# Moving one load, one pair of weights and one convolution in a fused graph layer on one core

## Chip, core and metric

The kernel runs on one core of one Trainium2 chip. The metric is the device time of one execution in microseconds (us), the median of seven executions: 1859.76 us before the change, between 1858.95 and 1863.57. All arithmetic is in f32.

## What is computed

There are 32 graphs of 512 nodes with 256 features each, and a dense 0/1 adjacency for each graph. The reference, cut to what matters:

```python
h = relu(layernorm(x))                                   # [32, 512, 256]
# convolution branch, channels first
c = relu(bn1(conv1(h.T)))                                # 256 -> 256, one tap
c = bn2(conv2(c))                                        # 256 -> 256, 17 taps
x_conv = relu(c + h.T).T
# message branch
s   = h @ w_se.T + b_se                                  # 3 numbers per node
A   = exp(-dist2(s, s)) * adj                            # [512, 512] per graph
msg = relu(h @ w_msg.T + b_msg)
x_nmp = A @ msg
# GRU cell on [x_conv, x_nmp] with state h
r, z = sigmoid(gi_r + gh_r), sigmoid(gi_z + gh_z)
n = tanh(gi_n + r * gh_n)
out = x + (1 - z) * n + z * h
```

## The kernel before

The 32 graphs are worked in two **groups** of 16 (`GB = 16`, `NG = 2`). conv2 is done in the frequency domain: each graph is cut into 8 windows, a group gives 128 windows, and each of 40 **units** (two of the 80 rows of a spectrum) is a product of the windows' spectrum with conv2's transformed weights. Each group goes through two stages, and a late stage over pairs of graphs (inverse transform, GRU gates, output) follows both:

1. `first_part(g, ...)`, lines 799 to 868. For each graph b: load x (`load_x`, line 116); `statistics` (line 280: four bn_stats, four aggregates and one addition on DVE, a power of -0.5 on POOL for the reciprocal deviation); `normalise` (four tensor_scalar on DVE, line 296); `transpose_h` (line 302: eight PE transposes named phT, two DVE copies into hT at line 308, a store of hT to HBM, called hd, at line 309); `conv1` (line 312: 16 matmuls named pc, two DVE additions at line 323, two ACT relus at line 324); `windows_to_freq` (matmuls named px). In group one, conv2's weights are transformed between the graphs (`weights_to_freq`: matmuls named pw, copies named wst on DVE and ACT, stores to wd in HBM). The loop runs ahead of itself: in turn b it does the statistics of b + 2, the transposes of b + 1, the normalisation of b + 2, and then conv1 of b.
2. `nodes(g, ...)`, lines 905 to 940, the **node loop**. It goes over the group's graphs, the last one first. For each graph: reload hT (`load_h`), rearrange it on ACT (`by_chunks`, tile hq), `message` (matmuls named pm, DVE additions), `features` (small DVE operations into the tiles fl and fr), `factors` (PE transposes named psl and psr), `affinity` (matmuls named pd, exp on ACT, DVE transposes of adj at line 471 and products at line 472 into A), `aggregate` (16 matmuls named pn), and a store (`save_nmp`, named nd). Between them go the units: `prepare` (POOL: one sum of the weights, wsum, line 351, and two of the spectra, both, lines 364 and 365) and `product` (12 matmuls named py, copy and sums into y, store yd on ACT's queue). Of group one's 40 units the loop does 36; the last four, 36 to 39, are **left over** and are done at the head of `first_part(1, ...)`, in the list `left`, whose five entries are run by `fill()`.

What sets the order of the work around the change:

- `first_part` stands under `tc.manual_schedule()`: each engine issues its instructions in the order of the code. `nodes` does not: there the framework's planner orders each engine's instructions by program order and by its own estimate of when each is ready, and may pull an instruction forward over many others.
- Loads of x 16 (group two's first graph), adj, hT and the units' weights (wt) all go through SP's queue, as do the stores of hT; yd and nd go through ACT's queue. A queue is served in order. Each transfer of SP and ACT is given the next of eight semaphores in turn, and is not issued before the last transfer on that semaphore has landed, whichever engine issued it.
- Tiles have few buffers: three for wt, so unit 38's weights can be loaded once unit 35's product is done; two for adj; two for hT.
- x 16 has a buffer of its own (pool "ahead"). In the code its load stands in front of the node loop (line 943), and its statistics behind the loop (line 946).

Of the kernel before, what the change touches and what calls it, by code (L numbers as in the profile page):

```python
# [65 lines left out]
def gnn_layer(  # L66
# [24 lines left out]
    GB = P // W  # L91
    NG = B // GB
# [23 lines left out]
    def load_x(b, queue=nc.sync):  # L116
        X[b] = pools["ahead" if b == GB else "first"].tile([P, NC, D], FP, tag="x", name=f"x_{b}", bufs=1 if b == GB else 3)
        queue.dma_start(X[b], x[b].rearrange("(c p) d -> p c d", p=P))
# [47 lines left out]
    def batch_norm(k, scale, shift, engine):  # L166
        engine.tensor_scalar(scale, at[k + "_v"], BN_EPS, None, op0=ALU.add)
        nc.gpsimd.tensor_tensor(scale, scale, minus_half[:, :DC], op=ALU.pow)
        engine.tensor_mul(scale, scale, at[k + "_g"])
        engine.tensor_mul(shift, at[k + "_m"], scale)  # L170
        engine.tensor_sub(shift, at[k + "_b"], shift)
# [28 lines left out]
    def shift_w1():  # L200
        nc.scalar.copy(shift1_row.rearrange("p (i q) -> p i q", i=DC), by_parity(row1[1][:, :D]))
# [78 lines left out]
    def statistics(b):  # L280
        stats = work.tile([P, NC, 6], FP, tag="stats", name=f"stats_{b}")
        mv = work.tile([P, NC, 2], FP, tag="mv", name=f"mv_{b}")
        for c in range(NC):
            nc.vector.bn_stats(stats[:, c, :], X[b][:, c, :])  # L284
        for c in range(NC):
            nc.vector.bn_aggr(mv[:, c, :], stats[:, c, :])
        rstd = work.tile([P, NC], FP, tag="rstd", name=f"rstd_{b}")
        STATS[b] = mv, rstd
        nc.vector.tensor_scalar(rstd, mv[:, :, 1], LN_EPS, None, op0=ALU.add)
        nc.gpsimd.tensor_tensor(rstd, rstd, minus_half[:, :NC], op=ALU.pow)  # L290
# [508 lines left out]
    def first_part(g, freq, between, left=()):  # L799


        b0, b1 = g * GB, (g + 1) * GB
        for b in range(b0, b0 + 3):
            if b not in X and (g == 0 or b == b0):
                load_x(b)
        if g == 0:
            t = XN[b0] = pools["first"].tile([P, NC, D], FP, tag="xn", name="rows", bufs=2)
            ones, diags = t[:, 0, :P], t[:, 1:3, :].rearrange("p i (c m) -> p i c m", m=P)
            nc.vector.memset(ones, 1.0)
            batch_norm("bn1", scale1, shift1, nc.gpsimd)  # L810
            bn1_row(0, scale1, ones, diags)
            bn1_row(1, shift1, ones, diags)
        if b0 not in STATS:
            statistics(b0)
        normalise(b0)
        if g == 0:
            scale_w1()
            shift_w1()
        else:
            load_x(b0 + 1)  # L820
            load_x(b0 + 2)
        left = list(left)

        def fill():
            for step in left.pop(0) if left else ():
                step()

        fill()
        transpose_h(b0)
        fill()  # L830
        statistics(b0 + 1)
        normalise(b0 + 1)
        fill()
        for b in range(b0, b1):
            if b + 3 < b1:
                load_x(b + 3, nc.gpsimd)
            if b == b0:
                conv1(b)
                if g == 0:
                    for steps in between(0):  # L840
                        for step in steps:
                            step()
                fill()
            if b + 2 < b1:
                statistics(b + 2)
            if b + 1 < b1:
                transpose_h(b + 1)
            if b + 2 < b1:
                normalise(b + 2)
            if b == b0:  # L850
                fill()
                xf = freq(g)
            one, two = between(b - b0) if b > 0 else ([], [])
            if b > b0:
                conv1(b)
            if b == b1 - 1:
                load_h(b0)
            for step in one:
                step()
            if b > b0:  # L860
                windows_to_freq(b - 1, xf)
            for step in two:
                step()
        by_chunks(b1 - 1)
        load_h(b0 + 1)
        windows_to_freq(b1 - 1, xf)
        by_chunks(b0)
        return xf
# [8 lines left out]
    with tc.tile_pool(name="freq", bufs=1) as fpool:  # L877
        def freq_tile(g):
            return fpool.tile([P, DC, L, P], FP, tag="xf", name=f"xf_{g}")

        with phase("first", "gen"):
            gen = pools["gen"]
            per = N // D
            steps = [partial(weights_to_freq, gen, pc, i) for pc in range(QI // PI) for i in range(0, PI, per)]
            load_w1()
            load_x(0)
            load_x(1)
            load_taps(gen, 0, nc.sync)

            def between(b):  # L890
                if b % 2 == 0 and b // 2 + 1 < QI // PI:
                    load_taps(gen, b // 2 + 1)
                if 1 <= b <= len(load_weights):
                    load_weights[b - 1]()

                mine = spread(steps, b, GB - 1) if b < GB - 1 else [partial(load_unit, 0, u) for u in range(3)]
                return mine[:1], mine[1:]

            with tc.manual_schedule():
                xf = first_part(0, freq_tile, between)  # L900


        LEFT = 4

        def nodes(g, xf, units, last):


            b1 = (g + 1) * GB
            todo = [b1 - 1] + list(range(g * GB, b1 - 1))
            def begin(i):  # L910
                if i < GB:
                    if todo[i] not in HQ:
                        by_chunks(todo[i])
                    message(todo[i])
                    features(todo[i])

            load_adj(todo[0])
            begin(0)
            factors(todo[0])
            begin(1)  # L920
            affinity(todo[0])
            for i, b in enumerate(todo):
                mine = spread(units, i, last) if i < last else []
                more = i + 1 < GB
                if i + 2 < GB and todo[i + 2] not in HT:
                    load_h(todo[i + 2])
                if more:
                    load_adj(todo[i + 1])
                    factors(todo[i + 1])
                for u in mine[:1]:  # L930
                    product(pools["pw"], g, u, xf)
                begin(i + 2)
                if more:
                    affinity(todo[i + 1])
                for u in mine[1:2]:
                    product(pools["pw"], g, u, xf)
                aggregate(b)
                save_nmp(b)
                for u in mine[2:]:
                    product(pools["pw"], g, u, xf)  # L940

        with phase("pw", "ahead"):
            load_x(GB)
            with phase("nodes"):
                nodes(0, xf, range(UNITS - LEFT), GB)
                statistics(GB)
            with phase("first", "sums"):
                combine = combine_weights()

                def between(b):  # L950

                    if b == GB - 3:
                        for u in range(3):
                            load_unit(1, u)
                    two = [partial(sum_unit, pools["pw"], 1, b - GB + 3)] if b > GB - 3 else []
                    return combine[b - 2] if 1 < b < len(combine) + 2 else [], two


                pw, (u0, u1, u2, u3) = pools["pw"], range(UNITS - LEFT, UNITS)
                left = [[],  # L960
                        [partial(prepare, pw, 0, u1, xf), partial(product, pw, 0, u0, xf), partial(load_unit, 0, u2)],
                        [partial(product, pw, 0, u1, xf), partial(load_unit, 0, u3), partial(prepare, pw, 0, u2, xf)],
                        [partial(prepare, pw, 0, u3, xf), partial(product, pw, 0, u2, xf)],
                        [partial(product, pw, 0, u3, xf)]]
                prepare(pw, 0, u0, xf)
                load_unit(0, u1)
                with tc.manual_schedule():
                    xf = first_part(1, freq_tile, between, left)
            with phase("nodes"):
                nodes(1, xf, range(UNITS), GB - 3)  # L970
# [76 lines left out]
```

## Time and profile before

| | |
|---|---|
| median of seven executions | 1859.76 us |
| the profiled execution | 1860.62 us |
| its span, first to last instruction | 1858.8 us |
| mean granted clock of PE | 0.992 |
| group one, first part (0 to 172 us) | PE busy 159.01 us, DMA share 0.88 |
| group one, node loop (172 to 469) | PE busy 291.35 of 297, DMA share 0.78 |
| group two, first part (469 to 592) | PE busy 118.64 of 123, DMA share 0.61 |
| group two, node loop (592 to 892) | PE busy 297.17 of 300, DMA share 0.83 |
| late stage (892 to the end) | PE busy 957.00 of 966.8, DMA share 0.35 |

PE is the matmul engine, DVE the vector engine, ACT the scalar engine, POOL the engine that does the units' sums, SP the engine that only issues transfers. In a timeline each row has its start and duration in us, the engine, the line of the code, the operation, what is written from what is read, the number of instructions merged, and in brackets how long the engine had been idle and who released it. In a table of windows each row has the window, its length, the busy time of PE, weight loads, DVE, ACT and POOL, then PEclk (the mean clock granted to PE, 1.00 is full speed), the DMA engines' share and GB/s.

### The profile page before, as it was taken

The numbers are of one execution on the slowest core, as the hardware profiler recorded it, in microseconds if no ns is written. First come the engines' busy times: TensorE is split into PE (matmuls) and PEld (weight loads), VectorE is DVE, ScalarE is ACT, GpSimd is POOL, SyncE is SP. The second block draws the span as 40 slices with busy tenths as digits, with TensorE's granted clock in tenths as the row PEclk, the third lists the DMA queues.
The fourth block names the chain that finished last, engine by engine and source line by source line (L and its number), as shares of the span: only waits on it lengthen the run. The fifth ranks groups of instructions, "written<-read, shape, count | busy, mean of one in ns | idle before, by whom it ended". The sixth has DMA issues, their size and how long they took to land.

```text
span 1858.8 us, 20075 instructions
## 1 busy us (share of the span) xinstructions
PE 1823.2 (98%) x6598; PEld 1090.1 (59%) x6598; DVE 1111.7 (60%) x2234; ACT 577.7 (31%) x1075; POOL 586.4 (32%) x565
## 2 busy tenths in 40 slices
PE   7999999999999999999999999999999999999998
PEld 5776666666798666666555544555455544555443
DVE  6875565555696564555165566645665466645666
ACT  3455444332145433333222212222122212222121
POOL 3331243343442344444413322132213322132221
PEclk9999999999999999999999999999999999999999
DMA  8998888866567988768513442244422442244312
GB/s 222 297 261 243 208 241 238 221 178 187 191 232 215 223 263 238 222 198 248 165 55 65 119 119 85 39 114 119 111 65 62 119 119 85 40 113 119 111 24 52
DMA packets 307451, 289.25 MB, mean 156 GB/s; under 512 B 148028, under 2 KB 237148, under 8 KB 306964
## 3 DMA queue, kind: packets, MB, share of 16 engines
q1 hardware_dynamic: 281300, 224.22, 45.3%
q10 hardware_dynamic: 19024, 38.68, 5.8%
q0 software_dynamic: 7024, 25.07, 4.8%
q8 instruction: 53, 0.87, 0.2%
q14 instruction: 50, 0.41, 0.1%
HBM read 191.50 MB, written 96.40 MB: 155 GB/s over the span
## 4 chain that ended last, share of the span: by engine, by line
PE 93%; DVE 2%; issue 2%; DMA 1%; POOL 1%; ACT 0%; POOLq 0%; ACTq 0%; SPq 0%; DVEq 0%
PE pg L585 29%; PE pn L585 14%; PE pn L480 12%; PE py L385 11%; PE pc L320 6%; PE pm L431 6%; PE pc L573 5%; PE px L335 4%; PE pw L256 2%; PE pd L466 2%; PE phT L307 2%; PE psr L455 1%; DMA x<-in_x_dram 1%; DVE stats L284 0%; DMA hT<-hd 0%
## 5 line engine op out<-in xcount | busy, mean ns | idle before, releaser
L480 PE MATMUL pn<-A,msg 128*128 128x512 f32 x512 | 225.0, 592 | 0.0
L585 PE MATMUL pg<-hp,sw 128*128 128x512 f32 x434 | 221.8, 593 | 0.7 <-DVE rz L604 0.5
L585 PE MATMUL pg<-np,sw 128*128 128x512 f32 x434 | 221.6, 592 | 0.0
L585 PE MATMUL pg<-cp,sw 128*128 128x512 f32 x434 | 221.6, 592 | 0.0
L563 POOL TENSOR_TENSOR hp<-hp 128x512 f32<-128x512 f32 x64 | 80.9, 1275 | 412.9 <-DMA hp<-hd 321.8
L364 POOL TENSOR_TENSOR both<-xf 128x256 f32<-128x256 f32 x78 | 60.9, 781 | 330.1 <-PE py L385 296.1
L480 PEld LDWEIGHTS pn<-A,msg 128*128 128x128 f32 x512 | 97.1, 190 | 110.6 <-issue 107.7
L385 PE MATMUL py<-wt,both 128*128 128x256 f32 x624 | 152.3, 387 | 4.0 <-POOL both L365 3.3
L563 POOL TENSOR_TENSOR cp<-cp 128x512 f32<-128x512 f32 x64 | 80.4, 1268 | 233.8 <-ACT cp L579 232.5
L600 ACT ACTIVATE rz<-rz,brz 128x512 f32<-128x512 f32 x93 | 67.0, 721 | 260.2 <-DVE rz L604 260.2
L392 DVE TENSOR_TENSOR y<-y,py 128x256 f32<-128x256 f32 x78 | 31.8, 408 | 193.5 <-ACT y L391 193.5
L585 PEld LDWEIGHTS pg<-hp,sw 128*128 128x128 f32 x434 | 82.2, 190 | 104.8 <-issue 98.3
L585 PEld LDWEIGHTS pg<-cp,sw 128*128 128x128 f32 x434 | 82.5, 190 | 103.8 <-issue 103.8
L585 PEld LDWEIGHTS pg<-np,sw 128*128 128x128 f32 x434 | 82.5, 190 | 103.8 <-issue 103.8
L385 PEld LDWEIGHTS py<-wt,both 128*128 128x128 f32 x624 | 115.1, 192 | 46.9 <-issue 27.6
L472 DVE TENSOR_TENSOR A<-e,at 128x512 f32<-128x512 f32 x128 | 112.4, 917 | 39.3 <-ACT e L469 38.9
L351 POOL TENSOR_TENSOR wsum<-wt 128x512 f32<-128x512 f32 x78 | 108.2, 1388 | 52.3 <-DMA wt<-wd 43.6
L320 PE MATMUL pc<-w,hT 128*128 128x256 f32 x512 | 121.1, 391 | 0.7 <-DVE hT L308 0.7
L723 ACT ACTIVATE nt<-nt,vech 128x512 f32<-128x512 f32 x64 | 46.2, 722 | 235.8 <-DVE nt L722 235.8
L431 PE MATMUL pm<-wmsg,hq 128*128 128x259 f32 x512 | 117.6, 382 | 1.0 <-ACT hq L417 1.0
L585 PE MATMUL pn<-cp,sw 128*128 128x512 f32 x224 | 114.4, 592 | 0.0
L585 PE MATMUL pn<-hp,sw 128*128 128x512 f32 x224 | 114.4, 592 | 0.0
(141 smaller groups left out, 2956.1 us busy)
## 6 DMA issues: line engine op xcount, KB each, us to landing
wt<-wd SPq DMA_DIRECT2D x160, 256.0 KB, 4.1
adj<-in_adj_dram SPq DMA_DIRECT2D x128, 256.0 KB, 5.6
wd<-wst SPq DMA_DIRECT2D x64, 320.0 KB, 5.2
yd<-y ACTq DMA_DIRECT2D x80, 256.0 KB, 4.0
yt<-yd SPq DMA_DIRECT2D x30, 640.0 KB, 7.4
hd<-hT SPq DMA_DIRECT2D x32, 512.0 KB, 3.9
nd<-nmp ACTq DMA_DIRECT2D x32, 512.0 KB, 3.8
xb<-in_x_dram SPq DMA_DIRECT2D x128, 128.0 KB, 3.7
```

The lines of the kernel that those rows point to most:

```text
L320: nc.tensor.matmul(p[:, j, :], HT[b][:, ic, c * P : (c + 1) * P], w1[:, ic, :], start=(ic == 0), stop=(ic == DC - 1))
L335: nc.tensor.matmul(p[:, j * 2 * L : (j + 1) * 2 * L], H1[b][:, c0 + j, ic * P : (ic + 1) * P], fwd, start=True, stop=True)
L351: nc.gpsimd.tensor_tensor(t, WT[g, u][:, 0], WT[g, u][:, 1], op=ALU.add)
L364: nc.gpsimd.tensor_tensor(both[:, 0], re, im, op=ALU.add)
L385: nc.tensor.matmul(dst, v[:, ic, :], w[:, ic, :], start=(ic == 0), stop=(ic == DC - 1))
L431: nc.tensor.matmul(p[:, : D + NS], hq[:, ic, c * P : (c + 1) * P], wmsg[:, ic, :], start=(ic == 0), stop=(ic == DC - 1))
L472: nc.vector.tensor_mul(A[b][:, mc, :], e, at)
L480: nc.tensor.matmul(p, MSG[b][:, mc, dc * P : (dc + 1) * P], A[b][:, mc, :], start=(mc == 0), stop=(mc == NC - 1))
L563: nc.gpsimd.tensor_tensor(t[:, dst, :], t[:, a, :], t[:, b, :], op=sub)
L573: nc.tensor.matmul(bk[:, t0:t1], YT[p][j][:, c, oc * P : (oc + 1) * P], back[:, n : n + t1 - t0], start=(c == 0), stop=(c == len(spans) - ...
L585: nc.tensor.matmul(bk[:, t], sw[:, k, q, o, :], terms[k][q][:, t], start=(first and i == 0), stop=(i == len(ks) - 1), skip_group_check=True)
L600: nc.scalar.activation(rz[:, g, j, :], src, AF.Sigmoid, bias=brz[:, g : g + 1], scale=1.0)
```

## The change

Three things are moved; no instruction is added or removed.

1. The load of x 16 goes from in front of the node loop into it, at its ninth turn (`i == GB // 2`), and its statistics go from behind the loop to the thirteenth turn (`i == 3 * GB // 4`).
2. In the list of left-over work, the load of unit 38's weights (`u2`) goes from the second entry into the first, which runs before the first transposes of group two and so before the first store of hT.
3. In group one's first part, conv1 of the second graph (b = 1) goes from behind the transposes of graph 2 and the normalisation of graph 3 to the beginning of its turn.

```diff
@@ first_part
                 fill()
+            if g == 0 and b == b0 + 1:
+                conv1(b)
             if b + 2 < b1:
                 statistics(b + 2)
             if b + 1 < b1:
...
             one, two = between(b - b0) if b > 0 else ([], [])
-            if b > b0:
+            if b > b0 + (g == 0):
                 conv1(b)
@@ nodes
                 more = i + 1 < GB
+
+                if g + 1 < NG and i == GB // 2:
+                    load_x(b1)
+                if g + 1 < NG and i == 3 * GB // 4:
+                    statistics(b1)
@@ the stages
-            load_x(GB)
             with phase("nodes"):
                 nodes(0, xf, range(UNITS - LEFT), GB)
-                statistics(GB)
...
-                left = [[],
-                        [partial(prepare, pw, 0, u1, xf), partial(product, pw, 0, u0, xf), partial(load_unit, 0, u2)],
+                left = [[partial(load_unit, 0, u2)],
+                        [partial(prepare, pw, 0, u1, xf), partial(product, pw, 0, u0, xf)],
```

## The prediction

> **What bounds the kernel.** I began with the page's busy line, went on to the waits of PE, and then to the timeline of each wait the diff touches.
>
> ```profile
> PE 1823.2 (98%) x6598; PEld 1090.1 (59%) x6598; DVE 1111.7 (60%) x2234; ACT 577.7 (31%) x1075; POOL 586.4 (32%) x565
> ```
>
> PE is busy 1823.2 of 1858.8 us, so nothing is won but by closing its gaps, 35.6 us in all, and the half-speed matmuls that follow some of them. The waits of PE (us in total, times, longest) name the gaps:
>
> ```profile
> PE psl L450 <- DVE fr L445: 5.7, 3, 3.7
> PE phT L307 <- DVE xn L296: 4.6, 2, 3.5
> PE py L385 <- POOL both L365: 3.3, 1, 3.3
> ```
>
> The longest of each row stands where one edit of the diff lies. **Gap A** (timeline, start and duration in us): after graph 1's transposes PE sits 3.53 us until xn of graph 2 is there, although graph 1's hT is complete at 23.99 and its conv1 waits behind the transposes.
>
> ```profile
> 22.71 1.28 DVE L308 TENSOR_SCALAR hT<-phT 128x512 f32<-128x512 f32 x2
> 24.57 2.30 PE L307 MATMUL phT<-ident,xn 128*128 128x128 f32 x8 [3.53 <-DVE xn L296]
> 26.67 5.47 PE L320 MATMUL pc<-w,hT 128*128 128x256 f32 x16
> ```
>
> **Gap B**, at the head of the first node loop: the load of x 16 leaves at 176.08 and takes 7.8 us; the planner put its bn_stats into the middle of graph 0's message additions; DVE stands there 3.93 us, and the features that psl needs come behind it.
>
> ```profile
> 176.08 0.43 SPq L118 DMA_DIRECT2D x<-in_x_dram  x1
> 183.88 0.43 DVE L284 BATCH_NORM_STATS2 stats<-x 128x6 f32<-128x256 f32 x1 [3.93 <-DMA x<-in_x_dram]
> 185.91 0.44 PE L450 MATMUL psl<-ident,fl 128*128 128x128 f32 x1 [3.66 <-DVE fr L445]
> ```
>
> **Gap C**, at the head of group two: the weights of unit 38 leave SP only at 474.76, behind h's store at 474.32; POOL waits 2.41 us for them, PE 3.28 us for POOL.
>
> ```profile
> 474.32 0.34 SPq L309 DMA_DIRECT2D hd<-hT  x1
> 474.76 2.49 SPq L347 DMA_DIRECT2D wt<-wd  x4
> 479.19 1.27 POOL L351 TENSOR_TENSOR wsum<-wt 128x512 f32<-128x512 f32 x1 [2.41 <-DMA wt<-wd]
> 481.88 3.78 PE L385 MATMUL py<-wt,both 128*128 128x256 f32 x8 [3.28 <-POOL both L365]
> ```
>
> **What a gap costs beyond itself.** Windows of the gap and of the stretch behind it (us, then the engines' busy time, PEclk, DMA share, GB/s):
>
> ```profile
> 182.20:185.90 3.70, 0.04 (x4) 0.03 (x1) 2.02 (x12) 1.77 (x4) 0.00 (x0) 0.75 1.21 201
> 185.90:190.40 4.50, 4.50 (x13) 3.79 (x14) 1.05 (x7) 1.90 (x5) 1.02 (x1) 0.50 1.22 193
> 478.60:481.90 3.30, 0.02 (x2) 0.02 (x1) 1.58 (x3) 1.23 (x2) 2.71 (x4) 0.86 0.59 224
> 481.90:487.30 5.40, 5.40 (x13) 4.22 (x14) 0.00 (x0) 0.00 (x0) 3.31 (x4) 0.50 0.28 97
> ```
>
> The granted clock is 0.50 behind both. From the mean clock inside a gap I get when it fell: B 1.8 us after PE went idle (0.75 = 1 - 0.5 x 1.85/3.7), C 2.4 us, A 2.6 us. Behind the 0.98 us wait at 209.14 it stays 1.00. So a gap near 1 us is free of it, one over 3 us is not.
>
> **Gap B, part by part.** Moved: one load of 512 KB on SP (0.43 us of issue), four bn_stats, four aggregates and an addition on DVE (1.40, 0.36 and 0.17 us), one pow on POOL (1.02 us). Without them DVE can finish the features as it did for graph 15, whose psl started 1.01 us after its last pm: 181.18 + 1.01 = 182.19, when pd ends (182.24). The wait of 3.66 us goes. The clock: from psl to the next pd PE took 194.22 - 185.91 = 8.31 us; the same work at full clock is 0.54 (psl to py of the next graph) + 1.73 (eight py, from 1.89 less the overlap) + 3.50 (pm in the chain) = 5.77, so 2.5 us more; 6.2 in all. Late next would be adj 15: its fourth load left at 179.88 and landed 9.4 us later, at 189.3; its transposes stood at 195.16 and would now want it at 189.0. But 512 KB of x are gone from in front of it, 2.6 us at the window's 201 GB/s, so it lands near 186.7. Bounds: 3.7 (only the wait) to 6.2. As adj is close, I take **-5.5**.
>
> **The same work in the loop.** The node loop is not under manual order, so I can't read the place where the planner puts it; program order says graph 7 for the load and 11 for the statistics, the hoisting seen at 183.88 says earlier. Either way it is past the burst of eight adj loads, and SP's adj, h and weight loads, POOL's both and wsum queue behind it. Cover: from 220 to 460 PE is busy 20.00 of every 20 us; features at 321.47 are used by psl at 333.66 (12 us of slack); A is made a whole graph ahead; a wsum finished at 340.73 is used near 343.2 (2.5 us); POOL waited 151.9 us for PE in 32 waits, so 1.02 us of pow is hidden, as are 1.9 us of DVE, busy 56% there. 512 KB more at a DMA share of 0.84 delays one weight load by some 2 us. Bounds 0 to +4.4 (the longest landing of an x, 9.1 us, less POOL's mean 4.7 us of waiting); nearest to the loop's own rows: **+0.3**.
>
> **Gap C.** Moved: two loads of 256 KB in front of one store of 512 KB on SP. The obvious sum, that they leave at 467 after the x loads, is wrong here: SP's row of waits says that h's store stood 7.3 us on the landing of nd, a store of ACT. In the program as built, SP's and ACT's transfers take eight semaphores in turn and each waits for the eighth before it. The first weight load takes the store's turn, and so its wait, until 474.3. It gains 0.44 us of issue and the store's 512 KB in front of it, 1.5 us at the 354 GB/s of 475 to 480; I take 1.5 of 1.9, since the transfers of ACT run beside it. Bounds: 0.44 and 2.4 (POOL's whole wait; then the pow of graph 17 holds POOL to 476.78). The gap of 3.28 becomes 1.8. Clock: from 478.60 to the next unit at 488.35 are 9.75 us; the work at full clock is 2.59 + 0.88 = 3.47 (469.81 to 472.40, 468.93 to 469.81), the wait 3.28, so 3.0 are the clock. A gap of 1.8 us is at the edge of the three falls (1.8, 2.4, 2.6); half is a fair share: 1.5. Together **-3.0**, between -0.4 and -5.4. Behind it nothing is new: unit 39 is ready 6.1 us after wsum 38 starts and wanted 6.4 us after. H's store goes 0.9 us later, and only the second node loop reads it.
>
> The Trainium skill, "TensorE: Matmul & The Clock Gate", Part 1, says that half rate comes after at least one idle window of about 3.4 us, and that the window runs freely. By it a gap of 1.8 us would never fall and C would give 4.5 us, 1.5 more; but by it the 3.28 us of C wouldn't have fallen either, and the trace shows 0.50 behind them, so the measured falls decide.
>
> **Gap A.** Moved: 16 matmuls, two additions on DVE (0.69 us each), two relus on ACT. PE can start conv1 at about 23.45, when the first half of hT is there. DVE decides what is left: additions done near 29.3 (the conv1's second half, part at clock 0.50), then statistics 3 (1.9 us), hT 2 to 32.5, xn 3 (1.46) to 34.0, and the wst copies that free the banks of the next weight step: 34.7 and 35.3. Its last matmuls end near 35.6; before they ended at 36.57. So the 3.5 us and the cold conv1 shrink to **-1.0**, by DVE; bounds: +0.5 (DVE that late again one graph on) and -2.3 (as if DVE never bound: phT would end at 29.8 against 32.15 for conv1). POOL's x load behind pow 3 goes 4 us later; x 5 is wanted at 46.
>
> **Sum**: -5.5 + 0.3 - 3.0 - 1.0 = -9.2 us. Against the profiled execution, 1860.62 us (span 1858.8 and 1.8 around it), that is 1851.4; that execution lies 0.86 over the median of 1859.76, so **1850.6 us** for the median.
>
> **Rivals.** (1) C keeps its clock penalty and gains only issue: -5.5 + 0.3 - 0.4 - 1.0 = -6.6, 1853.2. For: SP's 7.3 us; against: 512 KB less in front. (2) C closes, because the weight load does not inherit the wait for nd and leaves near 469: 0.9 us of gap left, no fall, so -5.4 there, and B at its full 6.2: -12.3, 1847.5. For it: the slot is free at about 469; against it: the turn of eight. (3) B turns into a wait on adj 15 long enough for the clock to fall: B yields 2 instead of 5.5, so -5.7, 1854.1. (4) **Slower**: the planner again puts x 16's statistics too early, now in the loop; DVE's addition and, behind it, POOL's pow hold the both of the next product. An x landing in 9.1 us plus 2.5 us of clock is 11.6 us, and 11.6 - 9.5 = +2.1: 1861.9. It decides from 9.5 us on, so only where all slack is gone; the loop's rows show 2.5 us at least. (5) The planner hoists the load to the old place, and B stays: -4.0, 1855.8; against: adj loads, ready and earlier in the program, go first.
>
> **Chances**: forecast 0.46, (1) 0.18, (2) 0.14, (3) 0.09, (4) 0.05, (5) 0.08. A measurement here tells 0.2%, 3.7 us, from no change. Faster by more: the forecast, (1), (2), (3) and a part of (5), 0.83 with something kept for what I don't see; within: 0.11; slower: 0.06. The range takes in (1), (2) and (3) and most of (5): 1846.8 to 1856.0; the forecast's own is 1848.5 to 1852.5.
>
> **What would show it.** B: no bn_stats with a wait for x near 184, psl within 0.5 us of pd, clock 1.00 at 183 to 190, pn of graph 15 some 6 us earlier against the conv stage's end. C: SP's first wt load right behind nd's landing, the store after it, PE's wait under 2.5 us. A: pc in front of phT at 23.5, and the waits of PE for wst a little longer. Wrong I would be if adj 15 holds the first transposes over 3 us, if the planner's new order puts a DMA wait of DVE or POOL into the loop, or if the first weight load doesn't stand on nd.

## The result, and the profile after

After the change one execution takes 1853.26 us (median of 16, from 1848.30 to 1859.82); before it, 1859.72 (38 executions, 1856.68 to 1867.09). The ratio is 0.9964, 95% interval [0.9954, 0.9974]: a gain of 6.5 us by the medians, and of 4.8 to 8.6 by the interval. The forecast was 1850.6, a gain of 9.2, with a range of 1846.8 to 1856.0. The profiled execution of the changed kernel took 1857.19 us (span 1855.4, mean granted clock 0.993), 3.9 us over its median. So the traces are compared stage by stage, not by their spans.

PE's busy row of the page after, and the rows of PE's waits after (us in total, times, longest):

```profile
PE 1822.4 (98%) x6598; PEld 1087.1 (59%) x6598; DVE 1109.5 (60%) x2234; ACT 577.8 (31%) x1075; POOL 587.1 (32%) x565
```

```profile
PE pc L320 <- DVE hT L308: 3.5, 2, 1.9
PE psl L450 <- DVE fr L445: 3.0, 3, 1.0
PE py L385 <- POOL both L365: 2.2, 1, 2.2
PE px L335 <- DVE h L323: 1.5, 1, 1.5
PE phT L307 <- DVE xn L296: 1.4, 1, 1.4
```

The three longest waits of before (3.66, 3.53 and 3.28 us) are gone or smaller. Of the first row 1.9 us stand in front of the moved conv1; the other 1.6 us, at the start of the kernel, lie in front of every edit. One row has grown, px on DVE's h, from 1.0 to 1.5 us. The diff does not touch that place, and the forecast does not speak of it.

**Gap B is gone.** Timelines after: SP issues the load of x 16 at 282 us, and its bn_stats follow at 291.54, with no wait for the DMA. The first of PE's two waits there, 1.01 us for the features of graph 15, is as long as before; the second is 1.02 us instead of 3.66, and the clock stays at full speed. The windows' last columns are PEclk, DMA share and GB/s.

```profile
282.12 0.38 SPq L118 DMA_DIRECT2D x<-in_x_dram  x1
291.54 0.40 DVE L284 BATCH_NORM_STATS2 stats<-x 128x6 f32<-128x256 f32 x1
179.71 0.30 PE L450 MATMUL psl<-ident,fl 128*128 128x128 f32 x1 [1.01 <-DVE fr L445]
186.05 0.30 PE L450 MATMUL psl<-ident,fl 128*128 128x128 f32 x1 [1.02 <-DVE fr L445]
```

```profile
183.90:186.05 2.15, 1.13 (x9) 0.33 (x9) 2.00 (x7) 0.00 (x0) 1.78 (x2) 1.00 1.14 217
186.05:192.30 6.25, 6.17 (x29) 4.88 (x29) 1.48 (x6) 4.97 (x11) 0.00 (x0) 1.00 1.23 191
```

**Gap C is smaller.** In SP's timeline the first two weight loads now stand in front of h's store. They leave at 471.88, where the store would have left: they took over its wait for nd, issued at 464.68 and landed 7.1 us later, at 471.81. POOL then waits 1.10 us for the weights instead of 2.41, and PE 2.15 us for POOL instead of 3.28.

```profile
471.88 0.83 SPq L347 DMA_DIRECT2D wt<-wd  x2
472.99 0.32 SPq L309 DMA_DIRECT2D hd<-hT  x1
475.40 1.45 POOL L351 TENSOR_TENSOR wsum<-wt 128x512 f32<-128x512 f32 x1 [1.10 <-DMA wt<-wd]
478.28 3.60 PE L385 MATMUL py<-wt,both 128*128 128x256 f32 x8 [2.15 <-POOL both L365]
```

**Gap A has changed its shape.** PE's timeline after: conv1 of graph 1 starts 3.4 us earlier than before (23.27 against 26.67). It runs mostly at half speed, though, and PE then waits for DVE's copies of the weights. The transposes of graph 3 stand at 35.97, against 36.51 before: 0.54 us are left. Conv1 of graph 0, in front of the edit, started 0.63 us later in this execution (12.58 against 11.95); counted from there, 1.2 us are won.

```profile
23.27 5.82 PE L320 MATMUL pc<-w,hT 128*128 128x256 f32 x16 [1.87 <-DVE hT L308]
34.95 1.09 PE L256 MATMUL pw<-w2p,taps 17*80 17x512 f32 x4 [0.57 <-DVE wst L263]
35.97 1.09 PE L307 MATMUL phT<-ident,xn 128*128 128x128 f32 x8
```

**A fourth gap, D.** In turn 7 of group one's first part `vectors()` runs on DVE, in front of conv1's additions. It copies bias columns (L159), adds them (L163), and makes bn2's scale and shift with a power on POOL in between (L167 to L171). After the change PE comes there 0.6 us earlier (conv1 of graph 7 starts at 83.20 instead of 83.80), and DVE no longer finds the vectors landed: the last of their four loads lands at 88.05, before the change at 88.02. DVE's timeline, PE's, and windows of the stretch behind:

```profile
88.14 0.18 DVE L159 COPY vech<-vec 64x28 f32<-64x28 f32 x1 [0.39 <-DMA vec<-in_vecs_dram]
89.40 0.16 DVE L169 TENSOR_TENSOR bn_scale<-bn_scale,vech 128x2 f32<-128x2 f32 x1 [0.81 <-POOL bn_scale L168]
89.88 1.29 DVE L323 TENSOR_TENSOR h<-pc,shift_row 128x512 f32<-128x512 f32 x2
```

```profile
90.62 1.41 PE L335 MATMUL px<-fwd,h 128*128 128x160 f32 x8 [1.49 <-DVE h L323]
92.35 4.50 PE L256 MATMUL pw<-w2p,taps 17*80 17x512 f32 x16 [0.32 <-ACT wst L265]
```

```profile
92.00:96.00 4.00, 3.68 (x17) 2.13 (x16) 1.04 (x2) 3.62 (x9) 0.00 (x0) 0.56 0.28 104
96.00:100.00 4.00, 4.00 (x14) 2.95 (x13) 3.76 (x13) 1.08 (x2) 0.47 (x1) 0.50 0.97 262
```

The additions of h start at 89.88, before the change at 89.94. Being early gained nothing here: PE waits 1.49 us instead of 0.95. In this execution the clock then stood at 0.50 from 92.5 until 102.7, and conv1 of graph 9 started at 109.51 instead of 106.72. The profiled execution lost 3.4 us here and was then 2.8 us behind the one before the change.

### The profile page after: what moved, and what is told of

The parts are those of the page before. It is cut to its first block, busy times and chain, and to the rows that moved or that the text cites. A ratio compares the mean times of both kernels' runs of the same rounds, so it can differ in the third digit from the quotient of the medians.

```text
span 1855.4 us, 20078 instructions
## 1 busy us (share of the span) xinstructions
PE 1822.4 (98%) x6598; PEld 1087.1 (59%) x6598; DVE 1109.5 (60%) x2234; ACT 577.8 (31%) x1075; POOL 587.1 (32%) x565
## 4 chain that ended last, share of the span: by engine, by line
PE 91%; DMA 3%; DVE 2%; issue 2%; POOL 1%; ACT 0%; SPq 0%; POOLq 0%; ACTq 0%; DVEq 0%
PE pg L585 29%; PE pn L585 14%; PE pn L480 11%; PE py L385 11%; PE pc L320 5%; PE pm L431 5%; PE pc L573 5%; PE px L335 3%; PE pw L256 2%; PE pd L466 2%; PE phT L307 1%; DMA hT<-hd 1%; DMA yd<-y 1%; PE psr L455 1%; DMA adj<-in_adj_dram 0%
```

## The experiments

Each kernel was timed beside the kernel before on the same chip. Differences to before are the distance of the ratio from 1, times 1860 us; kernels of different batches, and the one after the change, are compared by these ratios.

### First batch: each part alone, and the chain at 88 us

**conv1 moved alone** (e1_conv_only):

```diff
+            if g == 0 and b == b0 + 1:
+                conv1(b)
...
-            if b > b0:
+            if b > b0 + (g == 0):
                 conv1(b)
```

> Only conv1 of graph 1 is moved. Theory: PE reaches graph 3's transposes about 0.9 us earlier, but DVE's chain on the second batch norm's vectors at 88 us (from the copy into vech to the end of bn_shift 1.9 us, behind the landing of the vectors) stands at a fixed time; the gain is given back there, the PE gap at 88 to 92 us grows from 1.0 to about 1.5 us, and the time is that of before within 1 us, or up to 2 us more where the clock falls behind that longer gap. Rival: the 1.0 us of the prediction is kept, 1 us less.

Measured: 1860.36 us, ratio 1.0002 [0.9990, 1.0014]: no clear difference, between 1.9 us less and 2.6 more, which holds the rival's 1 us too. The theory's gap did not grow in this trace: the vectors landed in time (the last load at 87.80), PE waited 0.95 us for h at 90.42 as before the change, and the clock did not fall behind it.

**x 16 moved alone** (e2_x_only):

```diff
+                if g + 1 < NG and i == GB // 2:
+                    load_x(b1)
+                if g + 1 < NG and i == 3 * GB // 4:
+                    statistics(b1)
...
-            load_x(GB)
...
-                statistics(GB)
```

> Only the load of x 16 and its statistics are moved. Theory: the wait of DVE for x at 184 goes, psl of graph 0 comes 1.0 us behind pd instead of 3.7, the clock stays at 1.00; 4.5 to 5.5 us less than before. Rival (the wait only turns into another, and the clock falls anyway): 2 us less. The load is pulled into about the sixth graph of the loop, with no wait of DVE.

Measured: 1854.38 us, ratio 0.9969 [0.9957, 0.9981], 5.8 us less than before (3.5 to 8.0). This is the largest part.

**The weights of unit 38 alone** (e3_w_only):

```diff
-                left = [[],
-                        [..., partial(load_unit, 0, u2)],
+                left = [[partial(load_unit, 0, u2)],
+                        [...],
```

> Only unit 38's weights are moved in front of h's store. Theory: they still leave when nd of graph 14 has landed, 0.4 us earlier than before and without the store's 512 KB in front of them; PE's wait for unit 38 falls from 3.3 to about 2.2 us and the half-speed stretch behind it from 3.0 to 1.5 us or so: 2 to 3 us less. Rival (the weights leave as soon as the buffer is free, near 469): the wait is 0.9 us and 5 us are won.

Measured: 1859.31 us, ratio 0.9989 [0.9973, 1.0004]: 2.0 us less, between 5 less and 0.7 more. By the medians this is open; the stages below decide it. The three parts' differences, +0.4, -5.8 and -2.0, add up to -7.4; the whole change has -6.7 by its ratio.

**`vectors()` out of the way, first try** (e4_after_vec), put into the second node loop:

```diff
         load_vectors,
-        vectors,
     ]
...
                 more = i + 1 < GB
+                if g == 1 and i == GB // 2:
+                    vectors()
```

> The changed kernel, with the second batch norm's vectors computed in the second node loop instead of in front of conv1's additions of graph 7. Theory: the PE gap at 88 to 92 us goes, with it the fall of the clock behind it; 3 to 5 us less than the changed kernel, whose time also spreads less (now 1848 to 1860 us). Rival (the gap at 88 costs only its own 1.8 us): 2 us less and the same spread.

Measured: 1855.35 us, ratio 0.9974 [0.9962, 0.9985]: no faster than after the change. But the edit did not do what it says. The second node loop begins at 584 us, and DVE's timeline has the instructions at 86:

```profile
85.94 0.17 DVE L159 COPY vech<-vec 64x28 f32<-64x28 f32 x1 [5.59 <-DMA vec<-in_vecs_dram]
87.23 0.18 DVE L159 COPY vech<-vec 64x28 f32<-64x28 f32 x1 [1.12 <-DMA vec<-in_vecs_dram]
```

The planner, which orders the node loop, pulled them forward by some 500 us at the least, into the hand-ordered part. There they held DVE for 6.7 us in front of the copies of wst. The run tells nothing of the theory; it shows that a step must go where the order is written by hand.

### Second batch: the late chains one by one

**`vectors()` at the end of turn 8 of group two's first part** (e9_after_vec2), under manual order:

```diff
         load_vectors,
-        vectors,
     ]
...
+                    if b == 8:
+                        two = [vectors]
                     return combine[b - 2] if 1 < b < len(combine) + 2 else [], two
```

> The kernel after the change, with vectors() (its copies of the bias columns, their sum and bn2's scale and shift) taken out of group one's turn 7 and put at the end of turn 8 of group two's first part, where the order is written out by hand, so that no planner can pull it forward. Theory: its chain of seven small DVE instructions and one POOL power, in front of conv1's additions of graph 7, makes the PE wait for h at 88 to 91 us and, in part of the executions, the half-speed stretch behind it. Without it the wait for h of 1.5 us is gone, the clock stays at 1.00 from 88 to 104 us, conv1 of graph 9 starts about 3.5 us earlier than in the profiled execution after the change (109.5), and the time is 1 to 4 us under the kernel after the change (1853.3): 1849.5 to 1852.3. Rival: the additions are late by DVE's other work there; then the wait stays above 1 us and the time within 1 us of 1853.3.

Measured: 1848.54 us (5 executions, 1846.48 to 1849.46), ratio 0.9934 [0.9922, 0.9947], 12.3 us less than before. This interval lies below the one of the changed kernel, [0.9954, 0.9974]. PE's timeline and windows show that the gap and the half speed behind it are gone: the 16 px run in one piece, the clock is 1.00, and conv1 of graph 9 starts at 103.89.

```profile
88.20 2.44 PE L334 MATMUL px<-fwd,h 128*128 128x160 f32 x16
```

```profile
92.00:96.00 4.00, 4.00 (x26) 2.88 (x21) 3.67 (x13) 2.52 (x6) 0.00 (x0) 1.00 0.96 315
96.00:100.00 4.00, 4.00 (x25) 2.71 (x25) 3.95 (x9) 0.78 (x2) 3.87 (x6) 1.00 0.94 292
```

**The same without the move of conv1** (e10_noconv_vec2).

> The same as the run before it (vectors() in group two) but with conv1 of graph 1 at its old place; so the pair of runs shows what moving conv1 gives when the late chain at 88 us is not there to swallow it. Theory: the 0.6 us that conv1's move still had won at graph 7 now reaches the end: this run is 0.3 to 1.0 us slower than the one before it, and its conv1 of graph 9 starts 0.6 us later. Rival: conv1's move is swallowed at another place of group one's first part, or was worth a full 1 to 2.3 us: a difference of nothing, or over 1 us.

Measured: 1854.16 us (6 executions, 1850.51 to 1856.10), ratio 0.9962 [0.9948, 0.9977], 5.6 us slower than its partner by the medians of the same batch. That is more than either theory expected. The traces do not put it on conv1: the first aggregation of the node loop (pn) starts at 188.41 without the move and at 188.51 with it. This execution lost 3.75 us of its time in the rest of the loop, where PE has a wait of 0.58 us and the clock falls behind it; PE's timeline:

```profile
222.32 1.57 PE L465 MATMUL pd<-sr,sl 9*128 9x512 f32 x4 [0.58 <-DVE y L391]
223.83 3.60 PE L384 MATMUL py<-wt,both 128*128 128x256 f32 x8
```

Behind it lies a late reload of hT (ACT waited 4.75 us for it, in e9_after_vec2 2.69), which holds ACT's copy of y and then DVE's sum.

**Unit 38's weights on POOL's queue** (e7_after_wpool):

```diff
-    def load_unit(g, u):
+    def load_unit(g, u, queue=nc.sync):
...
-            nc.sync.dma_start(t[:, k], WD[2 * u + k
+            queue.dma_start(t[:, k], WD[2 * u + k
...
-                left = [[partial(load_unit, 0, u2)],
+                left = [[partial(load_unit, 0, u2, nc.gpsimd)],
```

> The kernel after the change, with the two weight loads of unit 38 issued from POOL's queue instead of SP's. Theory: on SP the first of them takes the place of h's store in the turn of semaphores and stands until nd has landed (472); from POOL's queue it does not, leaves when POOL reaches it after unit 36's sums, near 469, lands before 473, and POOL's sum for unit 38 has no DMA wait; PE's wait for both falls from 2.15 us to under 1.2 us and the half speed behind it goes: 1.5 to 3 us less than after the change, 1850.3 to 1851.8. Rival 1: the wait for nd comes along, because the buffer of unit 35 and not the turn of semaphores is what holds the load; then the wait stays and the time is within 1 us of 1853.3. Rival 2: the issue on POOL, two of about 1 us in front of its sums, holds the sums of unit 37: PE waits there instead, 0 to 2 us slower.

Measured: 1854.60 us (1847.07 to 1860.78), ratio 0.9964 [0.9949, 0.9979], no different from after the change. At its place the edit did what the theory said, and a little earlier: the load left at 465.96, in front of unit 36's sums and not behind them, PE's wait for both fell to 0.55 us, and the stretch from conv1 of graph 16 to that of graph 17 took 13.49 us, against 16.60. The execution lost more near 226 us, where PE waited 1.26 us for DVE's y and the clock fell; from pn of graph 15 to conv1 of graph 16 it took 281.02 us instead of 276.43.

**The copies into fl on ACT** (e8_after_flact):

```diff
-        nc.vector.tensor_copy(fl[:, :, :NS], st[:, 0])
+        nc.scalar.copy(fl[:, :, :NS], st[:, 0])
...
-        nc.vector.tensor_copy(fl[:, :, NS : 2 * NS], st[:, 1])
+        nc.scalar.copy(fl[:, :, NS : 2 * NS], st[:, 1])
```

> The kernel after the change, with the two copies into fl (the left features) on ACT instead of DVE. Theory: the copy that took 1.25 us in place of 0.17 on DVE while POOL made a sum of 128x512 beside it (184.49 us) is what PE still waits for at the first psl of the node loop (1.02 us); on ACT it takes under 0.6 us, the wait falls under 0.5 us and the time by 0.3 to 1 us, which the medians cannot tell; the evidence is the wait's row and the copies' mean over both loops. Rival: ACT, which makes the relus of the messages at the same time, is later than DVE; then PE's wait for the features grows to 1.5 us or more, and so the time.

Measured: 1859.30 us, ratio 0.9999 [0.9984, 1.0013]: the rival held. ACT's copy stands behind a rearrangement of hT that waits for its DMA, and psl comes 2.71 us late:

```profile
186.02 1.14 ACT L417 COPY hq<-hT 128x512 f32<-128x512 f32 x2 [4.18 <-DMA hT<-hd]
187.59 0.18 ACT L442 COPY fl<-st 128x12 f32<-128x12 f32 x1
188.45 0.47 PE L450 MATMUL psl<-ident,fl 128*128 128x128 f32 x1 [2.71 <-ACT fl L443]
```

### Third batch: combinations, and conv1's move twice more

These join edits shown above: after the change with `vectors()` in group two and POOL's queue for the weights (e11_after_vec2_wpool), the same without conv1's move (e12_noconv_vec2_wpool), the kernel before with `vectors()` in group two (e13_before_vec2), and that with conv1's move (e14_before_vec2_conv).

> The kernel after the change with both edits that closed a gap in their traces: vectors() in group two's first part, and unit 38's weight loads on POOL's queue. Theory: the two gaps are independent, the one at 88 us and the one at 476; with the first alone the time was 1848.5, the second shortened the stretch from conv1 of graph 16 to that of graph 17 by 3.1 us in its trace, so 1845.0 to 1846.5 here. Rival: what the POOL queue wins there is given back in the transfers of the second group or was never worth anything in the median (its run alone was at 1854.6, after the change 1853.3): 1848 to 1850.

> The same without the move of conv1. Theory: conv1's move wins PE nothing by itself, since the node loop's first store stood at the same place with and without it (188.6 against 188.7 us), and the 5.6 us between the two kernels of the batch before came from a short wait of PE on DVE's y at 222 us, behind a late landing of hT, and the half speed behind it, which is a matter of how the transfers fall: here the two kernels differ by less than 2 us. Rival: the move is worth 5 us wherever vectors() is out of the way: this run is at 1850 or more with the other at 1846.

> The kernel before with vectors() alone moved to group two. Theory: before the change the same chain stood in front of conv1's additions of graph 7 and cost PE 0.95 us and, in part of the executions, 1.5 us of half speed: 1 to 4 us less than before, 1855.5 to 1858.5. Rival: only together with the moved conv1 does the chain come too late; then nothing, within 1 us of before.

> The kernel before with vectors() in group two and conv1 of graph 1 moved. Theory that the move is worth nothing: within 1.5 us of the run before it. Theory that it is worth something once vectors() is out of the way: 0.6 us (what the trace showed it to keep until graph 7) to 5 us less than the run before it. PE's waits in front of the node loop, those for xn, hT and wst, say which: 4.8 us without the move, 5.1 with it, in the batch before.

| run | us (executions) | ratio to before |
|---|---|---|
| e11_after_vec2_wpool | 1848.86 (6) | 0.9948 [0.9927, 0.9969] |
| e12_noconv_vec2_wpool | 1849.49 (6) | 0.9943 [0.9925, 0.9960] |
| e13_before_vec2 | 1857.86 (12) | 0.9997 [0.9981, 1.0013] |
| e14_before_vec2_conv | 1857.13 (12) | 0.9994 [0.9979, 1.0008] |

Conv1's move shows no clear worth in either pair (0.6 and 0.7 us less with it, far inside the intervals). POOL's queue adds no gain to e9_after_vec2: the rival held. The traces of both runs with the queue show one place where its gain is given back. Timelines of e11_after_vec2_wpool, of PE, DVE and POOL:

```profile
472.63 1.99 PE L384 MATMUL py<-wt,both 128*128 128x256 f32 x8 [0.56 <-POOL both L364]
482.11 1.86 PE L306 MATMUL phT<-ident,xn 128*128 128x128 f32 x8 [3.16 <-DVE xn L295]
```

```profile
469.91 4.87 DVE L295 TENSOR_SCALAR xn<-x,mv,rstd 128x256 f32<-128x256 f32 x4 [1.14 <-POOL rstd L289]
```

```profile
469.86 1.25 POOL L350 TENSOR_TENSOR wsum<-wt 128x512 f32<-128x512 f32 x1
471.08 0.77 POOL L363 TENSOR_TENSOR both<-xf 128x256 f32<-128x256 f32 x1
471.81 0.77 POOL L364 TENSOR_TENSOR both<-xf 128x256 f32<-128x256 f32 x1
...
473.34 1.28 POOL L350 TENSOR_TENSOR wsum<-wt 128x512 f32<-128x512 f32 x1
```

The first wait is gone (0.56 us), but POOL now works at the same time as DVE's normalisation of graph 17. The four instructions of xn took 4.87 us instead of the 1.39 of the trace after the change, 3.5 us more; POOL's four sums filled some 4 us of that time (469.86 to 472.58, and 473.34 to 474.62). PE waits 3.16 us for the next xn instead of 1.35. In e12_noconv_vec2_wpool it is the same (4.89 and 3.15 us). The gap has moved a few microseconds on.

The kernel before with `vectors()` moved shows no gain in its median (theory: 1 to 4 us; rival: nothing). Its own stage got shorter, as the next table shows, but behind conv1 of graph 31, where no edit lies, its profiled execution took 1278.81 us against 1274.88. By the medians the theory is neither confirmed nor excluded (between 3.5 us less and 2.4 more).

### What each part is worth, by stages

Executions of one kernel differ by 3 to 15 us. The stages of the profiled executions tell more, stage B above all, where the lengths with and without the edit lie far apart. Each length is the difference of two starts in PE's timeline; graph 15 is the first that the node loop aggregates. The kernel with the fl copies on ACT is left out of row B, and the first try with `vectors()` out of the rows D. Where `vectors()` is in group two, its few small instructions lie in stage C.

| stage | kernels without the edit | kernels with it | difference |
|---|---|---|---|
| A: conv1 of graph 0 to that of graph 7 | 69.82 to 71.86, mean 70.80 (6) | 70.55 to 71.89, mean 71.05 (8) | +0.25 |
| D: conv1 of graph 7 to that of graph 9, `vectors()` in turn 7; edit: conv1 moved | 22.12, 22.92, 22.92 | 22.13, 22.41, 26.31, 26.59 | +1.7 in the mean |
| D: the same; edit: `vectors()` moved to group two | the seven of the row above | 20.27 or 20.28 in all six | -1.9 to -6.3 |
| B: first psl of the node loop to its first pn; edit: x 16 moved | 20.54 to 22.74, mean 21.42 (5) | 14.94 to 16.37, mean 15.31 (8) | -6.1 |
| Loop: first pn to conv1 of graph 16; edit: x 16 moved | 276.46 to 278.07, mean 277.05 (5) | 276.16 to 276.54 (6); 279.99, 281.02, 281.45 | -0.8, or +2.9 to +4.4; +0.7 in the mean of nine |
| C: conv1 of graph 16 to that of graph 31; edit: weights in front of h's store | 107.68 to 108.91, mean 108.35 (5) | 104.87 to 107.26, mean 106.56 (6) | -1.8 |
| C: the same; edit: weights on POOL's queue | | 103.65, 107.08, 107.77 | -0.6 to -4.7 |

A, D, B, C and the loop without the late reload add up to +0.25 + 1.7 - 6.1 - 1.8 - 0.8 = -6.75; with the loop's mean of all nine it is -5.2. The medians differ by 6.5. Row D rests on seven executions and on the chance of the clock in them. The stretch behind these stages, from conv1 of graph 31 to the end, takes 1274.9 to 1278.9 us in the fourteen traces, though no edit of the change lies in it.

## Why the prediction was right or wrong

**The sum** was 2.7 us too large (9.2 against 6.5); the sign and the largest part were right. The time measured, 1853.26 us, lies above the 1848.5 to 1852.5 of the forecast's own case and beside rival (1)'s 1853.2. That is luck: rival (1) has C gain 0.4 us and A win its 1.0, and by the stages C gained 1.8 and A nothing.

**Gap B: right, and a little more than taken.** -5.5 was forecast, with bounds of -3.7 and -6.2; the stage gave -6.1, the part alone -5.8 in the median. The half speed went with the wait, as the steps said: the clock falls at this place in all five traces without the edit and in none of the eight of row B with it. The feared next one, adj 15, was not late. In the profiled pair alone the stage fell only from 21.07 to 16.37. There a copy of features took 1.25 us instead of the usual 0.17 and PE waited 1.02 us for it, where the forecast had none.

**The same work in the loop: right.** Forecast +0.3, bounds 0 to +4.4; the mean of nine is +0.7, and without a late reload the loop is 0.8 us shorter. In three of nine executions with x 16 moved the reload of hT near 220 us was late, the clock fell for one step of 3.4 us behind it, and the loop was 2.9 to 4.4 us longer. One of five without the move had that wait too, 0.35 us long. Whether the earlier start of the loop makes it more frequent stays open.

**Gap C: right in its mechanism, mis-sized.** Forecast -3.0 (bounds -0.4 and -5.4), measured -1.8 over the stage. The weights inherited the store's wait for nd (it landed at 471.81, they left at 471.88), so rival (2) fell. It was not the buffer that held them: from POOL's queue, in e7_after_wpool, the same load left at 465.96, while SP's next transfer, h's store, stood until 471.80. PE's wait shrank from a mean of 3.30 us to 2.18 (five and six executions), 1.1 instead of 1.5. The clock gave the rest, less than the 1.5 taken: in the trace after the change it still falls at the wait of 2.15 us. From 478.28 to 482.60 the granted clock was 0.62 after the change:

```profile
478.28:482.60 4.32, 4.32 (x13) 3.51 (x14) 0.00 (x0) 0.09 (x1) 3.33 (x4) 0.62 0.47 165
```

**Gap A: wrong.** The step "the 3.5 us and the cold conv1 shrink to -1.0, by DVE" failed. Its working, that DVE decides and the copies of wst come next, was what the trace showed (wst waits 0.57 us), and the profiled pair even won the 1.2 us given above. But over fourteen executions nothing is left (+0.25). Two things stand behind it. The cold conv1 did not shrink: its 16 matmuls took 5.38 to 6.71 us with the move (mean 6.03, eight executions) and 4.32 to 5.48 without it (mean 4.97, six). And the forecast took its gap from one execution, which was a slow one: from conv1 of graph 0 to that of graph 2 it took 25.49 us, while the six without the move have 23.44 to 25.51, mean 24.43, and the eight with it 24.26 to 25.57, mean 24.75.

**What the forecast did not see: D.** It followed A up to 37 us and took what was left to reach the end. Some 50 us later stands a step that waits for a transfer. In three of four traces with conv1 moved and `vectors()` in turn 7, DVE waited 0.3 to 1.0 us for the vectors there; in e1_conv_only and in the three without the move it did not. That the move itself makes them late is not shown by so few. That the step costs time is: with `vectors()` in group two the stage took 20.3 us in all six. And a wait near 1 us was held to be free of the clock ("a gap near 1 us is free of it, one over 3 us is not"). Both halves of that sentence fell. Behind 0.95 us of wait conv1 of graph 9 came at the regular time in two of four executions (stage 22.12) and 0.8 us later in the other two. Behind 1.25 to 2.02 us it was later only by its longer wait in one of three (22.42); in the other two the clock stood at half for 10.2 us and the stage took 26.31 and 26.59 us. Behind the 3.30 us of gap C in e13_before_vec2 the clock did not fall.

By the means of the stages the move of conv1 cost 1.95 us (A and D) instead of winning 1.0. The medians don't tell: with the move against without it they differ by +0.4, -5.6, -0.6 and -0.7 us in the four pairs, and already the first pair's interval, from -1.9 to +2.6, holds -1.0. A and D with C's size, 2.95 and 1.2, less B's 0.6 and the loop's 1.1, make the 2.45 between the forecast's -9.2 and the stages' -6.75; with the loop's mean of nine it would be 4.0. So the sizes are known to 1 or 2 us and no better.

**The page on the clock.** The Trainium skill, "TensorE: Matmul & The Clock Gate", Part 1, says that half rate comes after at least one idle window of about 3.4 us. The traces show falls without one. In e10_noconv_vec2 the clock fell at 224.05 us, 2.3 us after the beginning of a wait of 0.58 us, with PE busy 2.83 of the 3.41 us before:

```profile
220.64:224.05 3.41, 2.83 (x10) 1.08 (x10) 2.20 (x10) 1.74 (x4) 0.00 (x0) 1.00 1.23 183
224.00:225.00 1.00, 1.00 (x3) 0.82 (x4) 0.68 (x6) 0.83 (x3) 0.00 (x0) 0.53 1.16 194
```

The same page says that the window runs freely, and here the traces agree. Their records of the granted clock hold 48 falls in the fourteen executions, the end of the kernel left out. Each lasts 3.41 us, or two or three times that, and in one trace all start on one grid of 3.41 us (before the change at 23.59, 95.27, 184.02 and 480.98 us: 21, 26 and 87 steps from one to the next). So the 1.8, 2.4 and 2.6 us of the forecast are not delays; they say where its three gaps lay on this grid. A fall costs, as an estimate, up to half of 3.41 us for each step. And the chance in it is, at least in part, where a wait falls on the grid. Before the change 2.4 of the 3.28 us of gap C lay in one step, and the clock fell; in e13_before_vec2 a wait of 3.30 us (471.81 to 475.11) lay across two steps, 1.8 us in one and 1.5 in the next, and it did not:

```profile
477.57:480.98 3.41, 1.03 (x5) 0.57 (x3) 2.58 (x6) 1.23 (x2) 1.79 (x2) 1.00 0.89 341
480.98:487.81 6.83, 5.93 (x16) 4.75 (x17) 0.00 (x0) 0.37 (x1) 4.23 (x6) 0.50 0.22 77
```

```profile
470.19:473.60 3.41, 1.62 (x8) 1.08 (x6) 3.16 (x8) 0.78 (x2) 1.18 (x1) 1.00 0.94 345
473.60:477.01 3.41, 1.90 (x9) 1.70 (x10) 0.00 (x0) 0.45 (x1) 3.38 (x5) 1.00 0.17 52
477.01:480.42 3.41, 3.41 (x22) 3.05 (x21) 1.98 (x6) 0.37 (x1) 1.47 (x3) 1.00 0.45 172
```

PE's busy share of a step does not decide alone: in the trace after the change the fall at 20.77 follows a step in which PE was busy 3.36 of 3.41 us. What decides, no run here shows.

**The best version** is e9_after_vec2, the change with `vectors()` moved to group two: ratio 0.9934 [0.9922, 0.9947]. Its median rests on five executions. How much of its gain over e10_noconv_vec2 is chance, the runs do not say.

## What to carry to other kernels

When a wait is closed, follow what it wins to the next step that waits for a transfer or for a slower engine: there it can be lost again. Take the size of a wait, and of the half speed behind it, from more than one execution. Where a kernel is part ordered by hand and part by a planner, move a step to a place whose order is fixed, or look in the trace where it has gone. When executions scatter more than the effect, compare the lengths of stages between fixed points: 15.3 against 21.4 us is plain where the times of whole executions overlap. Count every execution of a kernel in such a mean.

## What the runs showed of the hardware

**DVE and POOL hold each other.** A copy on DVE that reads and writes SBUF, the memory on the chip that the engines share, stood until POOL's instruction ended. The copy into fl at 184.49 took 1.25 us and ended at 185.74; POOL's two sums, from 183.15, ended at 185.70. Timelines after, DVE and POOL:

```profile
184.49 1.25 DVE L442 COPY fl<-st 128x12 f32<-128x12 f32 x1
185.65 0.17 DVE L444 TENSOR_SCALAR fr<-st 128x48 f32<-128x48 f32 x1
```

```profile
183.15 2.55 POOL L351 TENSOR_TENSOR wsum<-wt 128x512 f32<-128x512 f32 x2 [4.41 <-DMA wt<-wd]
```

The usual time of this copy is 0.17 us. It is the same in the 4.87 us of xn above. The other way round, POOL's wsum at 475.40 took 1.45 us instead of 1.27 where it began beside the end of xn (474.34 to 475.73). The Trainium skill, "GPSIMD Engine Reference", section "Specifications", says that GpSimd shares its SBUF interfaces with VectorE, with contention for some kinds of instructions. The runs agree, and show the price: 1.1 us for a copy, 3.5 us for four normalisations. An engine that comes free earlier can so slow another one that waits for nothing.
